# The front and the end of a mixture-of-experts stage: a skewed router, earlier weights, a list of places from batched 16-bit one-hots, and the last bias added per tile

## The chip, the core and the metric

The program runs on one core of a Trainium2 chip. The metric is device time in microseconds (us) of the whole program, the median of several executions. The engines are PE (TensorE, matrix products into the accumulators called PSUM; "PEld" is its weight load), DVE (VectorE), ACT (ScalarE), POOL (GpSimd) and SP (SyncE, which here only issues transfers). Transfers (DMA) are issued from the queues of SP, ACT and POOL; each engine works through its own queue in order.

## What is computed

A two-layer network on 4096 rows of 256 numbers with a 4096 x 4096 adjacency matrix. Each layer is a graph attention and a row-wise network, each added to its input:

```python
x = x + gat0(layernorm(x), adj)
x = x + ffn0(layernorm(x))          # 30 small steps, one 256 x 256 matrix
x = x + gat2(gat1(layernorm(x), adj), adj)
x = x + experts(layernorm(x))
```

The change is in the last line, which in full is

```python
rh = relu(f @ router_w1 + router_b1)
p = softmax(rh @ router_w2 + router_b2)          # 6 experts
top_w, top_i = top_k(p, 2);  r = softmax(top_w)
h1 = relu(f @ w1[e] + b1[e]);  h2 = relu(h1 @ w2[e] + b2[e])
o = h2 @ w3[e] + b3[e]
out = r[0] * o[top_i[0]] + r[1] * o[top_i[1]]
```

The kernel computes only the two experts that each row chose.

## The kernel before

The 4096 rows are 32 tiles (`NT`) of 128 (`P`), and eight groups (`NG`) of four tiles (`G`), 512 rows (`GR`) each. The kernel is a sequence of stages: attention (`attention`, called three times), the 30-step network between the first and second, and the experts. A scheduler of the language orders instructions within a stage on each engine; buffers come from pools, and a tile that takes the memory of an earlier pool waits for that pool's last users.

Four buffers named `rows` (`rows_in`, line 88) carry row groups. `load_ahead` (line 90) loads a group by `rows_of` (line 82), which puts row `r * 128 + p` of the group on partition p: four runs of 1 KB per partition. At the end of an attention, line 577 loads the first three groups of what follows.

The expert stage (lines 755 to 1147) has five parts.

**Router** (lines 761 to 859). All weights of the stage are loaded on ACT's queue when it begins: the router's (`rw1`, `rw2`, `rb2`), the biases as rows (`br`), the last bias (`b3`), and 18 transfers of 256 KB for the experts (`ew`). Then for each group: statistics (line 100 and on), the normalised rows `n` (line 837), their store to DRAM as `nd` (line 840), eight transposes on PE into the one buffer `tp` (line 113), a copy to `fT` on ACT (line 842), four PE instructions of the first product (line 845), `rh` on ACT (line 847), eight for the second (line 850), and the logits `lg` on DVE (line 853). All of a group is written down before the next group. `acc`, the stage's input kept for the residual, is loaded from DRAM a second time (line 859).

**Places** (lines 866 to 955). Softmax, the two greatest, their one-hots `hot`; the count of rows per expert by two products with a triangle and a matrix of ones (lines 896, 897); a running sum over the 32 tiles by doubling (lines 904, 905); and from these each row's place `pos` in a list sorted by expert, with every expert's part filled up to 256 places (`TR`), so 37 tiles (`T`) of 256 in all. `hi` and `lo` are the place's quotient and remainder by 128.

**List** (lines 957 to 979). The list is inverted by products: for each of 64 pairs (choice i, tile t), DVE writes a 128 x 128 one-hot of `lo` (line 961) and a 128 x 74 one-hot of `hi` times a code for the row (line 963), both in fp32, and PE adds their product to `ps_i` (line 966). From the sum come `source` (which row of `nd` to gather) and `dest` (which row of `yd` to scatter to). Beside it, lines 1003 to 1023 make `b3w`, the last bias weighted for each row, by transposing the weights and multiplying with `b3`.

**Experts** (lines 1032 to 1136). For each of 37 tiles: two gathers on POOL (line 1035), transposes (1047), a copy to `xT` on DVE (1049), copies of that tile's expert weights (1063), three layers on PE (1070, 1070, 1091) with `h` on ACT (1081) and on DVE (1083), a copy of the result to `ye` on ACT (1099), and two scatters to `yd` on POOL (1101). The loop is skewed: layer one of tile i, the last layer of tile i - 1, the transposes of tile i + 1, layer two of tile i. Every fourth tile, line 1136 adds a group of `b3w` to `acc`.

**Tail** (lines 1137 to 1147). For each group, two loads of `y` from `yd`, eight multiply-adds on DVE into `acc` (line 1144), and the store of the group; loads and stores are all on SP's queue, in this order.

Of the kernel before, what the change touches and what calls it, by code (L numbers as in the profile page):

```python
# [11 lines left out]
F32 = mybir.dt.float32  # L12
BF16 = mybir.dt.bfloat16
# [8 lines left out]
P = 128  # L22
# [22 lines left out]
def gnn_ffn_kernel(ctx: ExitStack, tc: tile.TileContext, a: dict, out: bass.AP):  # L45
# [44 lines left out]
    def load_ahead(src, g):  # L90
        t = rows_in().rearrange("p (r c) -> p r c", c=C)
        nc.sync.dma_start(t, rows_of(src, g))
        ahead[g] = t
# [77 lines left out]
    def attention(tag, src, norm, w, others, chunks, first, finish, following):  # L171
# [6 lines left out]
        with ExitStack() as scope:  # L178
# [343 lines left out]
            for at, (c, h, q) in enumerate(units):  # L522
# [52 lines left out]
                if at == len(units) - 8:  # L575
                    for g in range(3):
                        load_ahead(following, g)
# [29 lines left out]
    attention("g0", x, True, w0, [make, *makers], [4, 7, 7, 7, 7], True, to_rows(x1d, x), x1d)  # L607
# [128 lines left out]

    for n in range(2):
        attention(
            f"g{n + 1}",
            h1d if n else x2d,  # L740
            not n,
            gw[n],
            [],
            [8, 8, 8, 8],
            False,
            to_rows(x3d, x2d) if n else to_rows(h1d),
            x3d if n else h1d,
        )

# [5 lines left out]
    with ExitStack() as scope:  # L755
# [4 lines left out]
        RH = a["L1_ffn_router_w1"].shape[1]  # L760
        rw1 = one.tile([P, KC, RH], F32, name="rw1")
        nc.scalar.dma_start(rw1, a["L1_ffn_router_w1"].rearrange("(k p) f -> p k f", p=P))
        rw2 = one.tile([RH, E], F32, name="rw2")
        nc.scalar.dma_start(rw2, a["L1_ffn_router_w2"])
        rb2 = one.tile([P, E], F32, name="rb2")
        nc.scalar.dma_start(rb2, bcast_rows(a["L1_ffn_router_b2"]))
        NB = 1 + 2 * KC * E
        br = one.tile([NB, P], F32, name="br")
        nc.scalar.dma_start(br[:1], a["L1_ffn_router_b1"][None, :])
        for i in range(2):  # L770
            at = 1 + i * KC * E
            for k in range(KC):
                nc.scalar.dma_start(
                    br[at + k * E : at + (k + 1) * E], a[f"L1_ffn_expert_b{i + 1}"][:, k * P : (k + 1) * P]
                )
        b3 = one.tile([E, C], F32, name="b3")
        nc.scalar.dma_start(b3, a["L1_ffn_expert_b3"])
        ew = []
        for i in range(3):
            t = one.tile([P, E, KC, C], F32, name=f"ew{i}")  # L780
            src = a[f"L1_ffn_expert_w{i + 1}"]
            for e in range(E):
                nc.scalar.dma_start(t[:, e], src[e].rearrange("(k p) f -> p k f", p=P))
            ew.append(t)
        bT = one.tile([P, NB], F32, name="bT")
        acc = one.tile([P, NT, C], F32, name="acc")
        b3w = one.tile([P, NT, C], F32, name="b3w")
# [4 lines left out]
        source = one.tile([P, T2], I32, name="source")  # L792
        nd = dram.tile([N, C], F32, name="nd")
        yd = dram.tile([2 * N + T * TR, C], F32, name="yd")

        with ExitStack() as rs:
            work = rs.enter_context(tc.tile_pool(name="r_work", bufs=2))
            rone = rs.enter_context(tc.tile_pool(name="r_one", bufs=1))
            psum = rs.enter_context(tc.tile_pool(name="r_ps", bufs=1, space=PSUM))

            def bank(name):
                return psum.tile([P, 512], F32, name=name)


            def numbers(name, pattern, base, step):
                shape = [P] + [n for _, n in pattern]
                ti = rone.tile(shape, I32, name=f"{name}_i")
                nc.gpsimd.iota(ti, pattern=[list(x) for x in pattern], base=base, channel_multiplier=step)
                tf = rone.tile(shape, F32, name=name)
                nc.gpsimd.tensor_copy(tf, ti)  # L810
                return tf

            along = numbers("along", [(1, P)], 0, 0)
            place = numbers("place", [(P, T2)], 0, 1)
            code = numbers("code", [(-N, 2), (-P, NT)], 2 * N, -1)
# [5 lines left out]
            allp = rone.tile([P, P], F32, name="allp")  # L821
            nc.gpsimd.memset(allp, 1.0)

            ps = bank("ps_s")
            nc.tensor.transpose(ps[:, :NB], br, ident[:NB, :NB])
            nc.vector.tensor_copy(bT, ps[:, :NB])
            lg = rone.tile([P, NT, E], F32, name="lg")
            for g in range(NG):
                if g not in ahead:
                    load_ahead(x3d, g)  # L830
                t = ahead.pop(g)
                rstd, mv = over_std(work, t)
                nmr = work.tile([P, G], F32, name="nmr")
                nc.vector.scalar_tensor_tensor(nmr, mv[:, :, 0], -1.0, rstd, op0=OP.mult, op1=OP.mult)
                n = work.tile([P, G, C], F32, name="n")
                for r in range(G):
                    nc.vector.tensor_scalar(
                        n[:, r, :], t[:, r, :], rstd[:, r : r + 1], nmr[:, r : r + 1], op0=OP.mult, op1=OP.add
                    )
                nc.sync.dma_start(rows_of(nd, g), n)  # L840
                fT = work.tile([P, KC, GR], F32, name="fT")
                nc.scalar.copy(fT, transposed(psum, n))
                ps = bank("ps_r")
                for k in range(KC):
                    nc.tensor.matmul(ps[:RH], rw1[:, k, :], fT[:, k, :], start=(k == 0), stop=(k == KC - 1))  # L845
                rh = work.tile([RH, GR], F32, name="rh")
                nc.scalar.activation(rh, ps[:RH], AF.Relu, bias=bT[:RH, 0:1])
                ps = bank("ps_l")
                for r in range(G):
                    nc.tensor.matmul(  # L850
                        ps[:, r * E : (r + 1) * E], rh[:, r * P : (r + 1) * P], rw2, start=True, stop=True
                    )
                nc.vector.tensor_tensor(
                    lg[:, g * G : (g + 1) * G, :],
                    ps[:, : G * E].rearrange("p (r e) -> p r e", e=E),
                    rb2[:, None, :].to_broadcast([P, G, E]),
                    OP.add,
                )
                nc.sync.dma_start(acc[:, g * G : (g + 1) * G, :], rows_of(x3d, g))
# [32 lines left out]
            any_ = rone.tile([P, NT, E], F32, name="any")  # L892
            nc.vector.tensor_tensor(any_, hot[:, 0], hot[:, 1], OP.add)
            flat = any_.rearrange("p t e -> p (t e)")
            psw, pst = bank("ps_w"), bank("ps_t")
            nc.tensor.matmul(psw[:, : NT * E], before, flat, start=True, stop=True)
            nc.tensor.matmul(pst[:, : NT * E], allp, flat, start=True, stop=True)

            upto = [rone.tile([P, NT, E], F32, name=f"upto{i}") for i in range(2)]
            nc.vector.tensor_copy(upto[0], pst[:, : NT * E].rearrange("p (t e) -> p t e", e=E))  # L900
            step, src = 1, 0
            while step < NT:
                x_, y_ = upto[src], upto[1 - src]
                nc.vector.tensor_copy(y_[:, :step], x_[:, :step])
                nc.vector.tensor_tensor(y_[:, step:], x_[:, step:], x_[:, : NT - step], OP.add)
                step, src = 2 * step, 1 - src
            upto, other = upto[src], upto[1 - src]
# [6 lines left out]
                upto[:, NT - 1, :, None].to_broadcast([P, E, N // TR]),  # L914
# [6 lines left out]
            nc.vector.memset(first[:, 0:1], 0.0)  # L921
            for e in range(1, E):
                nc.vector.tensor_tensor(first[:, e : e + 1], first[:, e - 1 : e], tiles[:, e - 1 : e], OP.add)
# [11 lines left out]

            at_ = other
            nc.vector.tensor_tensor(at_, psw[:, : NT * E].rearrange("p (t e) -> p t e", e=E), upto, OP.add)
            nc.vector.tensor_tensor(
                at_, at_, pst[:, : NT * E].rearrange("p (t e) -> p t e", e=E), OP.subtract
            )  # L940
            nc.vector.scalar_tensor_tensor(
                at_, first[:, None, :].to_broadcast([P, NT, E]), float(TR), at_, op0=OP.mult, op1=OP.add
            )
            mine = rone.tile([P, 2, NT, E], F32, name="mine")
            nc.vector.tensor_tensor(mine, hot, at_[:, None].to_broadcast([P, 2, NT, E]), OP.mult)
            pos = rone.tile([P, 2, NT], F32, name="pos")
            nc.vector.tensor_reduce(pos, mine, axis=AX.X, op=OP.add)
            posi = rone.tile([P, 2, NT], I32, name="posi")
            nc.vector.tensor_copy(posi, pos)
            hii = rone.tile([P, 2, NT], I32, name="hii")  # L950
            nc.vector.tensor_scalar(hii, posi, 7, None, op0=OP.arith_shift_right)
            hi = rone.tile([P, 2, NT], F32, name="hi")
            nc.vector.tensor_copy(hi, hii)
# [224 lines left out]
```

## Time and profile before

| what | value |
|---|---|
| time, median of 3 | 3685.03 us (3678.46 to 3688.3) |
| span of the profiled execution | 3686.7 us |
| PE, DVE, ACT, POOL busy over the span | 91%, 81%, 72%, 30% |
| third attention's last matmul ends | 3238.7 us |
| first product of the router (L845) | 3275.7 us |
| last logits of the router (L853) | 3327.6 us |
| first one-hot of the list (L963) | 3346.4 us |
| last product of the list (L966) ends | 3408.0 us |
| first gather (L1035) | 3421.8 us |
| last scatter issued (L1101) | 3642.2 us |

How to read it: the busy shares are averages over all stages and say little of the last 450 us, where the limits change from stage to stage. The rows below the shares cut this part into stages. In the profile's groups a row gives the line, the engine, the operation with the tiles that it writes and reads, the shapes and the count; after the bar the busy time in us and the mean of one in ns; after the second bar the engine's idle time just ahead of these instructions, and what ended it. An fp32 product shows as two PE instructions. In tables by stretch, the granted clock of PE is a share of its full clock.

### The profile page before, as it was taken

The numbers are of one execution on the slowest core, as the hardware profiler recorded it, in microseconds if no ns is written. First come the engines' busy times: TensorE is split into PE (matmuls) and PEld (weight loads), VectorE is DVE, ScalarE is ACT, GpSimd is POOL, SyncE is SP. The second block draws the span as 40 slices with busy tenths as digits, with TensorE's granted clock in tenths as the row PEclk, the third lists the DMA queues.
The fourth block names the chain that finished last, engine by engine and source line by source line (L and its number), as shares of the span: only waits on it lengthen the run. The fifth ranks groups of instructions, "written<-read, shape, count | busy, mean of one in ns | idle before, by whom it ended". The sixth has DMA issues, their size and how long they took to land. (4 is left out here: it accounts for less than half of the span.)

```text
span 3686.7 us, 81508 instructions
## 1 busy us (share of the span) xinstructions
PE 3337.6 (91%) x33683; PEld 3024.9 (82%) x33683; DVE 3004.0 (81%) x6140; ACT 2641.2 (72%) x2947; POOL 1098.3 (30%) x892
## 2 busy tenths in 40 slices
PE   6889999988999999999988999999799999957994
PEld 5788898876888888888877989898688888835784
DVE  6899999988877777877777999999899999945334
ACT  2688888977666666666647999998799999921331
POOL 3211010007877777777730000000000000010672
PEclk8899999989999999999998999999999999975897
DMA  6897796411000000000051223030313313050225
GB/s 135 144 224 166 167 205 127 149 27 38 1 1 1 1 1 1 1 1 1 1 183 42 68 81 124 25 113 29 123 35 123 121 42 122 25 170 1 80 95 174
DMA packets 299656, 291.92 MB, mean 79 GB/s; under 512 B 97267, under 2 KB 255126, under 8 KB 299286
## 3 DMA queue, kind: packets, MB, share of 16 engines
q1 hardware_dynamic: 213856, 226.91, 18.9%
q0 software_dynamic: 73920, 52.97, 9.3%
q10 hardware_dynamic: 11510, 6.85, 0.7%
q8 instruction: 265, 4.34, 0.5%
q14 instruction: 105, 0.86, 0.1%
HBM read 251.42 MB, written 68.81 MB: 87 GB/s over the span
## 5 line engine op out<-in xcount | busy, mean ns | idle before, releaser
L565 PE MATMUL acc<-vals,m 128*128 128x130 f16 (+1 forms) x24576 | 1724.5, 231 | 127.8 <-DVE u L475 88.5
L565 PEld LDWEIGHTS <-m 128*128 128x128 bf16 x24576 | 1623.1, 98 | 215.2 <-issue 94.7
L464 ACT ACTIVATE st<-f1b,f2b 128x1024 bf16<-128x1024 f32 (+2 forms) x1664 | 1660.2, 1071 | 151.0 <-DVE m L533 143.4
L533 DVE TENSOR_TENSOR m<-st,m 128x2048 bf16<-128x2048 bf16 (+2 forms) x832 | 937.2, 1136 | 35.7 <-PE acc L565 28.2
L708 PE MATMUL po<-wT,zT 128*128 128x256 f32 x3840 | 874.7, 381 | 10.6 <-ACT zT L734 10.6
L708 PEld LDWEIGHTS po<-wT,zT 128*128 128x128 f32 x3840 | 714.4, 191 | 100.5 <-ACT zT L734 12.5
L694 POOL TENSOR_TENSOR th<-th,y 128x1024 f32<-128x1024 f32 x240 | 568.1, 2368 | 195.9 <-ACT th L693 195.2
L538 DVE TENSOR_TENSOR m<-m,m 128x2048 bf16<-128x2048 bf16 (+2 forms) x520 | 592.3, 1139 | 25.1 <-PE tp_m L217 0.5
L105 POOL TENSOR_TENSOR ln_rstd<-ln_rstd,mhalf 128x4 f32<-128x4 f32 x272 | 281.7, 1036 | 925.7 <-DVE ln_rstd L104 902.5
L100 DVE BATCH_NORM_STATS2 ln_st<-z 128x6 f32<-128x256 f32 x960 | 337.8, 413 | 191.3 <-ACT z L699 191.3
L734 ACT COPY zT<-tp 128x1024 f32<-128x1024 f32 x240 | 242.8, 1012 | 326.6 <-PE tp L113 326.6
L718 DVE SCALAR_TENSOR_TENSOR y<-po,ln_rstd,bias 128x256 f32<-128x256 f32 x928 | 378.7, 469 | 6.5 <-PE po L708 5.7
L699 ACT ACTIVATE z<-th 128x1024 f32<-128x1024 f32 x240 | 254.4, 1060 | 16.2 <-POOL th L694 16.2
L113 PE MATMUL tp<-ident,z 128*128 128x128 f32 x1920 | 251.9, 275 | 12.8 <-ACT z L699 12.8
L113 PEld LDWEIGHTS tp<-ident,z 128*128 128x128 f32 x1920 | 226.4, 142 | 39.7 <-ACT z L699 16.1
L693 ACT ACTIVATE th<-y 128x1024 f32<-128x1024 f32 x240 | 251.2, 1047 | 4.6 <-DVE y L718 4.5
L207 POOL DMA_DIRECT2D rows<-in_adj_dram x80 | 73.0, 913 | 488.5 <-PE tp_m L217 488.2
L447 POOL MEMSET hs<- 128x4 f32 x3 | 0.3, 103 | 630.1 <-DVE u L488 609.0
L305 PE MATMUL ph<-g_w,xT 128*128 128x264 f32 x384 | 113.5, 457 | 31.0 <-DVE v L375 27.7
L305 PEld LDWEIGHTS ph<-g_w,xT 128*128 128x128 f32 x384 | 85.2, 229 | 51.6 <-issue 16.6
L1035 POOL DMA_INDIRECT gx<-nd,source x74 | 74.6, 1008 | 161.4 <-DVE w L1063 125.2
L475 DVE TENSOR_TENSOR u<-acc,lo 128x520 f32<-128x520 f32 (+1 forms) x104 | 66.5, 653 | 48.4 <-ACT lo L474 48.3
(210 smaller groups left out, 2248.0 us busy)
## 6 DMA issues: line engine op xcount, KB each, us to landing
m<-edges SPq DMA_DIRECT2D x32, 2048.0 KB
rows<-in_adj_dram POOLq DMA_DIRECT2D x64, 448.0 KB, 7.8
edges<-ms SPq DMA_DIRECT2D x64, 448.0 KB
m<-edges SPq DMA_DIRECT2D x16, 1792.0 KB
f1b<-fd SPq DMA_DIRECT2D x32, 512.0 KB
rows<-x1d SPq DMA_DIRECT2D x16, 512.0 KB
y<-yd SPq DMA_DIRECT2D x16, 512.0 KB
f1b<-fd SPq DMA_DIRECT2D x16, 448.0 KB
```

The lines of the kernel that those rows point to most:

```text
L100: nc.vector.bn_stats(st[:, r, :], src[:, r, :])
L105: nc.gpsimd.tensor_tensor(rstd, rstd, mhalf, OP.pow)
L113: nc.tensor.transpose(ps[:, k, r * P : (r + 1) * P], src[:, r, k * P : (k + 1) * P], ident)
L464: nc.scalar.activation(st[:, s, :w], f1b[c, h][:, :w], AF.Relu, bias=f2b[:, 2 * q + s, h : h + 1], scale=BIG)
L533: nc.vector.tensor_tensor(m1[:, :, :w], st[:, :, :w], m, OP.logical_and if turned(q) else OP.min)
L538: nc.vector.tensor_tensor(m2[:, :, :w], m, m1[:, :, :w], OP.subtract)
L565: nc.tensor.matmul(acc[:, i, cols], lhs[:, s, rows], v[:, cols], start=(j == 0 and n_ == 0), stop=(j == NT - 1 and n_ == 1), skip_group_ch ...
L693: nc.scalar.activation(th[at], y[:, g * G : (g + 1) * G, :], AF.Tanh, scale=0.01)
L694: nc.gpsimd.tensor_tensor(th[at], th[at], y[:, g * G : (g + 1) * G, :], OP.add)
L699: nc.scalar.activation(z, th.pop(at - 1), AF.Silu, scale=0.01)
L708: nc.tensor.matmul(po[:, r, :], src[:, k, r * P : (r + 1) * P], wT[:, k, :], start=(k == 0), stop=(k == KC - 1),)
L718: nc.vector.scalar_tensor_tensor(y[:, g * G + r, :], po[:, r, :], rstd[:, r : r + 1], last if end else bias, op0=OP.mult, op1=OP.add,)
```

## The change

- Router: its loop runs over `NG + 2` steps. Step g takes the statistics of group g, the rest up to the transposes of group g - 1, and the products of group g - 2; the transposes have two PSUM buffers. `acc` is made by ACT from the rows in hand, with -1 added, instead of a second load.
- Weights: the router's weights and the bias rows are loaded after the 30-step network in program order, into the memory of the first attention's weights `w0`. The 18 expert loads and `b3` follow the router's loop on SP's queue.
- Rows: `runs_of` replaces `rows_of` for what this stage reads and writes: row `4 p + r` of a group on partition p, one run of 4 KB per partition.
- Places: the running sum is one scan instruction over experts and tiles, in bf16; the starts of the experts' parts are a scan too.
- List: four batches of 16 tiles. Each makes all its one-hots in three DVE instructions, and a row's code is two 16-bit numbers kept as one 32-bit word; PE then does 64 products in fp16.
- Last bias: `b3` is held on all partitions, and DVE adds the tile's row of it where ACT copied the result to `ye`. The weighted bias `b3w` goes, with its products and line 1136.
- Tail: the loads of `y` run up to three groups ahead of the sums (8 buffers for 6), and the stores go to ACT's queue.

The diff, cut to its core:

```diff
+    RH = a["L1_ffn_router_w1"].shape[1]
+    rw1 = w0[:, :, :RH]
+    nc.sync.dma_start(rw1, a["L1_ffn_router_w1"].rearrange("(k p) f -> p k f", p=P))
...
+    def runs_of(t, g):
+        return t[g * GR : (g + 1) * GR, :].rearrange("(p r) c -> p r c", r=G)
...
-            x3d if n else h1d,
+            [x3d, runs_of] if n else [h1d],
...
+            ps_t = rs.enter_context(tc.tile_pool(name="r_pst", bufs=2, space=PSUM))
...
+            for g in range(NG + 2):
+                if 1 <= g and g + 2 < NG and g + 2 not in ahead:
+                    load_ahead(x3d, g + 2, runs_of)
+                if g < NG:
+                    rows[g] = ahead.pop(g)
+                    stds[g] = over_std(work, rows[g])
+                if 2 <= g:
+                    ps = bank("ps_r")
+                    fT = fTs.pop(g - 2)
...
+                    rh = rhs[g - 2] = work.tile([RH, GR], F32, name="rh")
+                    nc.scalar.activation(rh, ps[:RH], AF.Relu, bias=bT[:RH, 0:1])
+                if 1 <= g <= NG:
+                    u = g - 1
...
+                    nc.sync.dma_start(runs_of(nd, u), n)
+                    fT = fTs[u] = work.tile([P, KC, GR], F32, name="fT")
+                    nc.scalar.copy(fT, transposed(ps_t, n))
+                    nc.scalar.activation(acc[:, u * G : (u + 1) * G, :], t, AF.Identity, bias=mone)
...
+            for i in range(3):
+                src = a[f"L1_ffn_expert_w{i + 1}"]
+                for e in range(E):
+                    nc.sync.dma_start(ew[i][:, e], src[e].rearrange("(k p) f -> p k f", p=P))
+            nc.sync.dma_start(b3, bcast_rows(a["L1_ffn_expert_b3"]))
...
-            while step < NT:
-                x_, y_ = upto[src], upto[1 - src]
-                nc.vector.tensor_copy(y_[:, :step], x_[:, :step])
-                nc.vector.tensor_tensor(y_[:, step:], x_[:, step:], x_[:, : NT - step], OP.add)
...
+            nc.vector.tensor_tensor_scan(flat[1], flat[0], flat[0], 0.0, OP.add, OP.max)
...
+            for b in range(2 * NT // HB):
+                i, t0 = b // 2, b % 2 * HB
+                here = slice(t0, t0 + HB)
+                ohl = work.tile([P, P, HB], F16, name="ohl")
+                nc.vector.tensor_tensor(
+                    ohl, along16, lo[:, i, None, here].to_broadcast([P, P, HB]), OP.is_equal
+                )
+                ohh = work.tile([P, T2, HB], F32, name="ohh")
+                nc.vector.tensor_tensor(
+                    ohh, along16[:, :T2], hi[:, i, None, here].to_broadcast([P, T2, HB]), OP.is_equal
+                )
+                nc.vector.tensor_tensor(ohh, ohh, words[:, i, None, here].to_broadcast([P, T2, HB]), OP.mult)
+                two = ohh.bitcast(F16).rearrange("p n (t w) -> p n t w", w=2)
+                for t in range(HB):
+                    nc.tensor.matmul(
+                        psi[:, : 2 * T2],
+                        ohl[:, :, t],
+                        two[:, :, t, :],
...
-            nc.scalar.copy(y, po)
+            nc.vector.tensor_tensor(y, po, b3[:, bass.DynSlice(which[i], 1)].to_broadcast([P, 2, C]), OP.add)
...
-                nc.vector.scalar_tensor_tensor(acc[:, g], b3w[:, g], -1.0, acc[:, g], op0=OP.add, op1=OP.add)
...
+        for g in range(NG + 3):
+            if g < NG:
+                ys[g] = [back(g, i) for i in range(2)]
+            if 3 <= g:
...
+                nc.scalar.dma_start(runs_of(out, g - 3), acc[:, (g - 3) * G : (g - 2) * G, :])
```

## The prediction

> **What bounds the kernel now.** I read the busy table in 40 slices first, then the chain of waits, then a table of stages over the last 450 us, then groups and timeline of each stage. Everything edited here runs after the third attention's last matmul at 3238.7 us, apart from eight small loads. So only this table counts (columns: stretch, its length, busy us and count of PE, PEld, DVE, ACT, POOL, then granted clock, DMA share, GB/s):
>
> ```profile
> 3238.70:3260.00 21.30, 4.75 (x41) 3.30 (x38) 16.51 (x63) 1.84 (x3) 6.07 (x19) 0.61 0.59 181
> 3260.00:3275.60 15.60, 0.00 (x0) 0.00 (x0) 2.02 (x10) 1.00 (x1) 1.01 (x1) 0.50 1.09 360
> ...
> 3310.00:3327.50 17.50, 14.20 (x51) 7.54 (x49) 0.36 (x2) 4.09 (x5) 0.00 (x0) 0.76 0.06 22
> 3327.50:3345.00 17.50, 1.63 (x5) 1.14 (x4) 14.47 (x55) 0.59 (x2) 0.00 (x0) 0.54 0.00 0
> 3345.00:3365.00 20.00, 18.63 (x62) 13.30 (x63) 12.28 (x52) 2.16 (x3) 0.00 (x0) 0.50 0.00 1
> ...
> 3441.00:3500.00 59.00, 59.00 (x294) 51.93 (x293) 24.77 (x45) 21.99 (x43) 41.56 (x42) 1.00 0.29 92
> ...
> 3642.00:3686.70 44.70, 0.00 (x0) 0.00 (x0) 25.95 (x64) 0.00 (x0) 0.97 (x1) 0.51 0.86 287
> ```
>
> Five stages: **router** 3238.7 to 3327.5 (88.8 us; PE does nothing in 3260 to 3275.6 while DMA is full); **places** to the first one-hot at 3346.4 (18.9, DVE alone); **list** to the first gather at 3421.8 (75.4, PE full at half clock); **experts** to the last scatter at 3642.2 (220.4, PE full at full clock); **tail** to 3686.7 (44.5, DMA).
>
> Why the router stands still is in the waits and the timeline:
>
> ```profile
> ACT fT L842 <- DMA ew<-in_L_ffn_expert_w_dram: 26.7, 1, 26.7
> PE ps_r L845 <- DMA ew<-in_L_ffn_expert_w_dram: 21.3, 1, 21.3
> ...
> 3252.36 22.14 ACTq L783 DMA_DIRECT2D ew<-in_L_ffn_expert_w_dram  x18
> ```
>
> The copy fT sits on ACT's queue behind 18 expert-weight issues that took 22 us. Groups for the list and the tail:
>
> ```profile
> L1014 PE MATMUL tp<-b,wT 6*128 6x256 f32 x64 | 36.3, 690 | 1.4 <-ACT wT L1011 1.4
> L966 PE MATMUL ps_i<-ohh,ohl 128*128 128x74 f32 x128 | 35.2, 425 | 0.0
> L1144 DVE SCALAR_TENSOR_TENSOR acc<-y,ws,acc 128x256 f32<-128x256 f32 x64 | 26.0, 479 | 18.2 <-DMA y<-yd 18.2
> ```
>
> The list's PE time is half the list (L966), half the last bias (L1014), which was interleaved with it and also ran on after it until 3420.9.
>
> [...] PE was busy 20.00 of 20 us in 3365 to 3385 and kept 0.50. So I don't count on a full clock. [...] 1218 ns for L533 at 128x2048 bf16 near the end, 690 for 520 fp32 [...]. [...] the trace shows 352 ns for 192 elements, as for tensor_tensor. [...] with 1 KiB rows the tail's middle moved 337 to 374.
>
> **The change part by part.**
>
> *Router, skewed, weights early.* The eight small loads go to SP near 120 us, where SP has room (no issue of its between 117.9 and 124.7): nothing. The expert weights move from ACT to SP: five of 18 ahead of the first nd write, the rest between and behind the nd writes. What is queued behind them on SP is nd and rows; the five are 1.3 MB, 3.6 us at 360 GB/s, and the first nd is not ready sooner than some 5 us after they can start (3245.7, when the first load of that stage starts now). The eight acc loads go; ACT makes acc (128x1024, 1.01 us as L842).
> DVE per group, from its rows divided by 8: statistics 1.50 (L100), 0.38 (L102), 0.17 (L104), 0.16 (L834), n 1.40 (L837), lg 0.18: 3.8 us. Eight groups are 30 us, and the closing of attention on DVE (L475 to L595) 5.7.
> ACT per group: 1.01 + 0.69 + 1.01 = 2.7, hidden.
> PE per group cold: 3.61 (L845 x4) + 1.06 (L850 x8) + 1.7 (L113 x8) = 6.4. Warm, by the FFN's rows: L708 takes 228 ns per 256 columns, so 4 x 512 columns 1.8; transposes 251.9/240 = 1.05; ps_l 0.5: 3.4. Now a period is 6.8 (3301.57 to 3308.38) since fT and rh stand in PE's way; the skew and the second tp buffer remove that. The clock was 0.74 to 0.76 in the last half of the stage; I take 5.3 per group, between 3.8 (DVE) and 6.4 (PE cold).
> The built order has about 17 DVE instructions ahead of n of group 0, so transposes start near 3249; 8 x 5.3 = 42; the last rh, ps_l and lg add 2 to 3: end near **3294**, 33 saved (bounds: 3238.7 + 36 + 3 waits + 6 tail = 3284; 3249 + 51 + 3 = 3303).
>
> *Places.* Ten instructions of the doubling scan (1.6 + 0.9), the PSUM copy (0.4), five of `first` (0.8) and at_ in three go; two scans, a subtraction, the copy of ends, count and shift come. No row shows a scan; [...]. Two matmul groups become four on bf16. ex, ohe, sel and bsel stay in the gaps in the built order. I take 2.3 saved (1 to 4). POOL's constants (2048 elements, about 1.8 us for iota and 1.7 for the cast, extending the rows of 235 and 293 ns at 128) run beside the router.
>
> *List.* Out: 128 DVE one-hots (20.1 + 18.1 us), 128 PE instructions, all of L1009 to L1021. In: four batches, each ohl 2048 elements of 16 bits, 1.2 us [...], ohh 1184 with fp32 output 1.4, and its product 1.4: 4.0, so 16 for four. Of the 64 matmuls only the last 16 come after DVE; [...] I take 3.2. Then lst to source 1.6 (now 2.5), gather 0.6: 16 + 0.7 (ohl waits for PE once) + 3.2 + 1.6 + 0.6 = **22**, against 75.4: 53 saved (bounds 20 and 29). The gather no longer waits for L1014, as PE's last work is the list itself.
>
> *Experts.* PE sets 5.62 per tile: 1.73 + 1.73 + 0.44 + 1.73 by starts at 3501.12, 3502.85, 3504.58, 3506.30, 3506.74. The bias addition replaces ACT's ye (0.59) by about 0.69 on DVE, between w and xT. Queued behind it is xT, for which PE's next first layer waits: po done at 3506.5, ye to 3507.25, xT to 3507.95, needed at 3508.47. Half a microsecond is left, so nothing. L1136 (9.7 us of DVE) goes, hidden but two of eight ahead of source. 0 (from +4 to -2).
>
> *Tail.* 12.6 MB move, 8 MB in, 4 out. Loads now run up to four groups ahead and aren't queued behind stores, which go to ACT's queue; rows are 4 KiB. [...] DVE needs 26 + 4 + 4. From 3644.9 that is 37.5 instead of 41.8: 4.3 saved (1 to 7).
>
> Sum: 33 + 2.3 + 53 + 0 + 4.3 = 93; 3685 - 93 = **3592 us**.
>
> **Rivals.** (A) *Router stays PE-bound and cold, list dearer* [...]: router to 3303, list 29, tail 2: 24 + 1 + 46 + 2 = 73: 3612. For: 0.50 in the list; against: 0.76 in the router and a PE with fewer gaps. (B) *PE warms up and DVE bounds*: router to 3286, list 20, tail 7: 41 + 3 + 55 + 7 = 106: 3579. [...] against: it would then be idle for a third of the time. (C) *ye on DVE joins the loop*: it waits for the scatter of three tiles before, and xT and the next PE work stand behind it. If a scatter's 2.4 us to landing came into each period, 37 x 2.6 = 96 is given back: 3592 + 96 = 3688, slower. For: ACT's ye has 21.0 us of idle put down to that DMA; against: ACT started ye within 0.1 us of po's end, and three tiles are 16.8 us.
>
> **How the numbers follow.** Forecast 0.58, A 0.23, B 0.16, C 0.03. Same needs 3674 to 3696, so most of C falls there or beyond. Range 3568 to 3618: from beyond B, with the 5 us that runs of one kernel differ, to beyond A. Faster 0.97, same 0.01, slower 0.02.
>
> **What would show it.** No idle stretch of PE at the router's start and no wait on ew; eight periods near 5 us at a clock over 0.6; one-hots as 12 DVE rows, ohl near 1.2 us; first gather 88 us earlier, near 3333; 5.62 per tile; a tail under 40 us. Wrong if ew or b3 lands after source, if ohl takes over 2 us, or if a period of the experts grows.

## The result and the profile after

The changed kernel takes **3589.92 us** (median of four runs, 3589.64 to 3591.94), the kernel before beside it 3686.23 (3678.46 to 3688.3). The ratio is 0.9744, with a 95% interval of 0.9727 to 0.9761. The prediction was 3592.

The table of stretches after, with the same columns as before (length, busy us and count of PE, PEld, DVE, ACT, POOL, then granted clock, DMA share, GB/s):

```profile
3240.50:3253.20 12.70, 5.11 (x42) 3.45 (x39) 12.67 (x47) 7.00 (x8) 2.70 (x3) 0.68 0.41 120
3253.20:3265.00 11.80, 10.24 (x31) 6.14 (x31) 6.73 (x28) 3.39 (x4) 9.86 (x25) 0.64 0.68 245
3265.00:3275.00 10.00, 8.98 (x50) 6.07 (x48) 7.02 (x32) 6.00 (x8) 2.30 (x3) 0.97 0.54 191
3275.00:3291.60 16.60, 14.81 (x75) 9.20 (x74) 5.19 (x24) 7.01 (x9) 1.03 (x1) 1.00 0.92 300
3291.60:3307.30 15.70, 0.69 (x4) 0.27 (x4) 14.22 (x45) 0.59 (x2) 0.00 (x0) 0.54 0.13 50
3307.30:3327.70 20.40, 8.86 (x64) 8.22 (x64) 16.84 (x21) 0.80 (x2) 0.01 (x1) 0.58 0.00 1
...
3347.00:3406.00 59.00, 59.00 (x295) 52.09 (x294) 28.68 (x53) 15.92 (x33) 41.40 (x43) 1.00 0.29 94
3548.00:3587.70 39.70, 0.00 (x0) 0.00 (x0) 26.22 (x64) 0.00 (x0) 1.04 (x2) 0.51 0.83 324
```

The stretch in which PE did nothing (3260 to 3275.6 before) is gone: from 3253 on PE is busy for 34 of 38 us, and its clock is at 0.97 or more from 3265. The list is down to one row of 20.40 us, in which DVE is busy for 16.84 and PE for less than half. The experts are as before, 59.00 of 59.00. In the tail 324 GB/s are moved instead of 287.

The waits from 3236 to 3350 (engine and waiting row, releaser, us in total, times, longest) no longer name ew:

```profile
ACT w L1076 <- DVE source L1005: 29.3, 1, 29.3
DVE lg L848 <- PE ps_l L845: 19.2, 8, 4.4
ACT rh L824 <- PE ps_r L822: 18.4, 8, 3.9
PE ps_r L988 <- DVE ohh L985: 15.1, 4, 10.3
...
PE tp L113 <- DVE n L833: 8.0, 7, 4.1
```

In the router DVE and PE now wait for one another: lg, which stands ahead of the next n on DVE, waits for ps_l, and the transposes wait for n. PE's wait on ohh says that DVE now sets the pace of the list. Groups of the tail (L1160), the experts (L1112) and the list:

```profile
L1160 DVE SCALAR_TENSOR_TENSOR acc<-y,ws,acc 128x256 f32<-128x256 f32 x64 | 26.2, 479 | 10.8 <-DMA y<-yd 10.6
L1112 DVE TENSOR_TENSOR ye<-po,b 128x512 f32<-128x512 f32 x37 | 25.6, 692 | 48.2 <-DMA yd<-ye,dest 33.7 <-PE po L1104 14.5
...
L988 PE MATMUL ps_r<-ohh,ohl 128*128 128x148 f16 x64 | 8.9, 304 | 15.1 <-DVE ohh L985 15.1
...
L985 DVE TENSOR_TENSOR ohh<-ohh,code 128x1184 f32<-128x1184 f32 x4 | 5.6, 1388 | 0.1
L982 DVE TENSOR_TENSOR ohh<-along,hi 128x1184 f32<-128x1184 f16 x4 | 5.5, 1385 | 0.0
...
L978 DVE TENSOR_TENSOR ohl<-along,lo 128x2048 f16<-128x2048 f16 x4 | 4.9, 1219 | 0.0
```

ohl, whose second operand is broadcast, takes 1219 ns for 2048 elements; L533 in the kernel before, with none, took 1218 for as many. The tail's sums wait 10.8 us instead of 18.2.

To compare runs, each is cut at six marks: the start of ln_st after its last wait for L565 (the end of attention for DVE), the start of lmax, the first one-hot, the first gather, the last scatter, and the span's end. (The prediction put the router's end 0.3 us ahead of lmax's start. It also calls 3238.7 the end of attention's last matmul; PE's records of L565 run on to 3240.5 there, and 3238.7 is the first mark, where DVE's wait for them ends.) Lengths in us, good to 0.1:

| kernel | router | places | list | experts | tail | time; before on the same chip |
|---|---|---|---|---|---|---|
| before | 89.1 | 18.6 | 75.4 | 220.4 | 44.5 | 3686.23 |
| after | 51.3 | 15.5 | 20.4 | 220.7 | 39.3 | 3589.92; 3686.23 |
| unskewed | **56.8** | 15.5 | 20.4 | 230.1 | 38.5 | 3607.63; 3701.52 |
| ew_on_act | **65.0** | 15.5 | 20.5 | 228.5 | 38.4 | 3618.15; 3701.52 |
| list_pairs | 49.1 | 15.5 | **30.7** | 229.3 | 38.3 | 3611.06; 3701.52 |
| rows_1kb | 51.6 | 15.6 | 20.3 | 228.7 | **41.2** | 3600.41; 3701.52 |
| tail_old | 51.4 | 15.5 | 20.4 | 220.5 | **45.5** | 3601.92; 3691.48 |
| ye_on_act | 51.8 | 15.6 | 20.4 | **220.2** | 39.0 | 3593.52; 3691.48 |
| ye_twice | 51.4 | 15.6 | 20.4 | **221.0** | 38.7 | 3587.38; 3691.48 |
| warm_pe | **49.7** | 15.6 | 20.4 | 219.3 | 38.6 | 3592.82; 3691.48 |
| unskewed_act | **75.5** | 15.5 | 20.4 | 229.9 | 39.9 | 3620.21; 3700.3 |
| xT_twice | 49.7 | 15.5 | 20.4 | **233.7** | 39.0 | 3596.16; 3700.3 |
| best | **47.6** | 15.6 | **23.8** | 230.9 | 38.7 | 3593.54; 3700.3 |
| router_old | **85.6** | 15.6 | 20.4 | 220.5 | 39.2 | 3621.42; 3684.84 |

Bold is the stage that an edit touches. All but best and the first two rows are single runs, so totals are not compared, only stages. Two things are seen ahead of any edit. The untouched router of list_pairs, rows_1kb, tail_old, ye_on_act, ye_twice and xT_twice takes 49.1 to 51.8, so a difference of 2 us there is not read as an effect of an edit. And the experts take about 9 us longer in every run on the two chips on which the kernel before takes over 3700: an edit of the experts is compared only with runs of its own chip.

The trace's record of the granted clock shows what goes with the router's spread. In all seven routers of the changed kernel's form the clock rises to 1.00 some 18 us after the first mark. At 49.1 and 49.7 (list_pairs, xT_twice) it stays there; at 51.3 to 51.8 (the changed kernel and the other four) it falls back to 0.50 once more, 3.4 us later and for 3.4 us. Two stretches of the changed kernel, the second of which holds that fall:

```profile
3260.00:3262.00 2.00, 0.96 (x4) 0.63 (x5) 2.00 (x6) 0.59 (x1) 2.00 (x7) 1.00 0.00 0
3262.00:3264.00 2.00, 2.00 (x4) 0.63 (x3) 2.00 (x11) 0.00 (x0) 1.35 (x12) 0.55 0.68 246
```

### The profile page after: what moved, and what is told of

It reads as the page before. It is cut to its first block, busy times and chain, and to the rows that moved or that the text cites. A ratio compares the mean times of both kernels' runs of the same rounds, so it can differ in the third digit from the quotient of the medians.

```text
span 3587.7 us, 81089 instructions
## 1 busy us (share of the span) xinstructions
PE 3264.7 (91%) x33523; PEld 2981.2 (83%) x33523; DVE 3002.9 (84%) x6039; ACT 2615.2 (73%) x2902; POOL 1100.6 (31%) x899
## 3 DMA queue, kind: packets, MB, share of 16 engines
q1 hardware_dynamic: 198770, 224.18, 19.2%
## 5 line engine op out<-in xcount | busy, mean ns | idle before, releaser
L565 PE MATMUL acc<-vals,m 128*128 128x130 f16 (+1 forms) x24576 | 1726.6, 232 | 128.2 <-DVE u L475 89.0
L565 PEld LDWEIGHTS <-m 128*128 128x128 bf16 x24576 | 1625.2, 98 | 215.6 <-issue 95.5
L533 DVE TENSOR_TENSOR m<-st,m 128x2048 bf16<-128x2048 bf16 (+2 forms) x832 | 938.1, 1137 | 37.0 <-PE acc L565 28.4
L708 PE MATMUL po<-wT,zT 128*128 128x256 f32 x3840 | 875.1, 381 | 10.3 <-ACT zT L734 10.1
L708 PEld LDWEIGHTS po<-wT,zT 128*128 128x128 f32 x3840 | 715.8, 192 | 99.8 <-ACT zT L734 12.4
L538 DVE TENSOR_TENSOR m<-m,m 128x2048 bf16<-128x2048 bf16 (+2 forms) x520 | 592.8, 1140 | 25.1 <-PE tp_m L217 0.5
L699 ACT ACTIVATE z<-th 128x1024 f32<-128x1024 f32 x240 | 254.5, 1060 | 18.5 <-POOL th L694 18.2
L1076 ACT COPY w<-ew 128x512 f32 x37 | 22.7, 617 | 132.8 <-PE ph L1083 103.5
```

The source lines that it names most:

```text
L533: nc.vector.tensor_tensor(m1[:, :, :w], st[:, :, :w], m, OP.logical_and if turned(q) else OP.min)
L538: nc.vector.tensor_tensor(m2[:, :, :w], m, m1[:, :, :w], OP.subtract)
L565: nc.tensor.matmul(acc[:, i, cols], lhs[:, s, rows], v[:, cols], start=(j == 0 and n_ == 0), stop=(j == NT - 1 and n_ == 1), skip_group_ch ...
L699: nc.scalar.activation(z, th.pop(at - 1), AF.Silu, scale=0.01)
L708: nc.tensor.matmul(po[:, r, :], src[:, k, r * P : (r + 1) * P], wT[:, k, :], start=(k == 0), stop=(k == KC - 1),)
```

## The experiments

Every edit is made on the changed kernel.

### The router: four parts put back one by one

**unskewed**: before's loop body, with one buffer for the transposes.

```diff
-            for g in range(NG + 2):
-                if g < NG:
-                    stds[g] = over_std(work, rows[g])
...
+            for g in range(NG):
+                rstd, mv = over_std(work, t)
...
+                nc.scalar.copy(fT, transposed(psum, n))
```

> Router loop as one group after the other, with one buffer for the transposes; the early weights, ew on SP's queue and all else stay. Theory (the skew and the second buffer take fT and rh out of PE's way): the period goes back from 4.2 towards the 6.8 us of the kernel before, so the router takes 60 to 66 us instead of 51.1, and the total grows by 9 to 15. Rival 1 (moving the loads off ACT's queue is the whole gain of the router): the router stays at 51 to 54. Rival 2 (the order of the loop is the whole gain): it goes back to about 85.

Measured 56.8 instead of 51.3: 5.5 us (5.0 to 7.7 against all the untouched routers), below what the theory expected and above the first rival. The loop's order, with its second buffer, was worth less than I had thought. The built program of unskewed already has the next group's transposes ahead of ps_l, so part of what the skew does was there without it.

**ew_on_act**: the weights' issues back on ACT's queue, ahead of the router loop.

```diff
+            for i in range(3):
+                src = a[f"L1_ffn_expert_w{i + 1}"]
+                for e in range(E):
+                    nc.scalar.dma_start(ew[i][:, e], src[e].rearrange("(k p) f -> p k f", p=P))
             lg = rone.tile([P, NT, E], F32, name="lg")
...
-                    nc.sync.dma_start(ew[i][:, e], src[e].rearrange("(k p) f -> p k f", p=P))
```

> The 18 expert-weight loads and b3 are issued from ACT's queue ahead of the router loop, as in the kernel before; the skew and the early router weights stay. Theory (fT stands behind the issues on ACT's queue): fT of the first group waits until ACT has issued 18 loads, near 3270 instead of 3252, and the router takes 65 to 72 us instead of 51.1. Rival (the skewed loop hides it): at most 54 us. The other stages keep their lengths within half a microsecond.

Measured 65.0, 13.7 us more: the theory's lower edge. Its waits from 3240 to 3320 show before's chain again, shorter:

```profile
ACT fT L844 <- DMA ew<-in_L_ffn_expert_w_dram: 18.3, 1, 18.3
...
PE ps_r L828 <- ACT fT L844: 12.8, 1, 12.8
```

The two edits together cost 19.2 of the 37.8 us between the kernels, which left half of the router's gain open. So both were undone at once.

**unskewed_act**:

> Both router edits undone at once: one group after the other with one transpose buffer, and the 18 expert-weight loads and b3 issued from ACT's queue ahead of the loop. Alone they cost 5.5 us (56.6 instead of 51.1) and 13.7 (64.8). What still differs from the kernel before are the early router weights and acc made by ACT instead of eight 1 KB-run loads on SP's queue. Theory A (the edits add): 69 to 72 us, and the remaining 17 to 20 up to 88.8 belong to the acc loads and the router weights. Theory B (only the skew lets the second group's DVE and PE work run while fT waits, so both together cost more than the sum): 78 to 88.

Measured 75.5, that is 24.2 us: 5.0 more than the sum of 5.5 and 13.7, between the two theories. Taken from an untouched router of 49.1 instead of 51.3, the excess would be 2.8. So the skew does seem to hide some of the wait. Still 13.6 us were missing to 89.1.

**router_old**: unskewed_act, and acc by DMA.

```diff
-                nc.scalar.activation(acc[:, g * G : (g + 1) * G, :], t, AF.Identity, bias=mone)
...
+                nc.sync.dma_start(acc[:, g * G : (g + 1) * G, :], runs_of(x3d, g))
```

> unskewed_act (75.3 us of router, by the end of attention's last matmul to lmax) with acc loaded again from x3d, eight DMAs of 512 KB on SP's queue inside the loop, instead of being made by ACT from rows; the subtraction of 1 that ACT did on the way is left out of the computation. Of before's router only its weights' place on ACT's queue (7 small issues ahead of ew) is then missing. 13.5 us are left between 75.3 and 88.8. Theory (4.2 MB more at the 350 GB/s that these stretches move are 12 us, and DMA is full while fT waits): 84 to 89. Rival 1 (the acc loads run beside the work, and the router weights' way is what is left): 75 to 78. Rival 2 (half each): 79 to 83.

Measured 85.6, 10.1 us more: the theory. Its waits from 3240 to 3330:

```profile
PE ps_r L831 <- ACT fT L828: 30.7, 8, 22.7
...
ACT fT L828 <- DMA ew<-in_L_ffn_expert_w_dram: 22.7, 1, 22.7
```

In unskewed_act the same wait of fT was 15.9 us; with the eight acc loads it is 22.7, before it was 26.7. DVE's waits for rows grow too, from 7.6 us in all to 12.9. So the acc loads cost their time by slowing other transfers: the weights whose issues hold up ACT, and the rows. The router's 37.8 us then are: order alone 5.5, queue alone 13.7, both together 5.0 on top, acc loads 10.1, and 3.5 that were not taken apart (the small weights on ACT's queue, 1 KB rows). Each is a difference of single runs, which for an untouched router differ by up to 2.7.

### The list: the pairs without the bias products

**list_pairs**:

```diff
-                nc.vector.tensor_tensor(
-                    ohl, along16, lo[:, i, None, here].to_broadcast([P, P, HB]), OP.is_equal
-                )
...
+                    nc.vector.tensor_scalar(ohl, along, lo[:, i, t : t + 1], None, op0=OP.is_equal)
...
+                        ohh, along[:, :T2], hi[:, i, t : t + 1], code[:, i, t : t + 1], op0=OP.is_equal, op1=OP.mult
```

> The list is made from 64 pairs of fp32 one-hots, each with its own two DVE instructions and its fp32 product, as in the kernel before; the products for the last biases (b3w) stay out. Theory (both edits of the list are worth about half of the 55 us): the list takes 42 to 52 us instead of 20.4. Rival 1 (dropping the bias products is nearly all): 22 to 30. Rival 2 (the batches are nearly all): 65 to 75.

Measured 30.7, just above the first rival's range: of the list's 55.0 us, leaving out the bias products gave 44.7 with the pairs as they were, and the 16-bit batches 10.3 after that. The other order, batches with the bias products kept, was not run. An estimate for it: PE would still have the 46.1 us of bias products (below) and the 8.9 us of the new ones, so the batches alone could give at most some 20 of the 75.4 us. Either way the larger part belongs to the bias products, as far as this estimate goes. My theory was wrong, and the groups of this run from 3311.2 to 3342 show why:

```profile
L976 PE MATMUL ps_r<-ohh,ohl 128*128 128x74 f32 x128 | 27.6, 422 | 7.0 <-DVE ohl L971 7.0
...
L973 DVE TENSOR_SCALAR ohh<-along,hi,code 128x74 f32<-128x74 f32 x64 | 20.2, 315 | 0.0
L971 DVE TENSOR_SCALAR ohl<-along,lo 128x128 f32<-128x128 f32 x64 | 17.9, 281 | 0.0
```

The two DVE groups add up to 38.1 us, but the stretch from the first one-hot to the last product is 28.1. The timeline of DVE (start, us) tells how that goes together:

```profile
3335.03 0.32 DVE L973 TENSOR_SCALAR ohh<-along,hi,code 128x74 f32<-128x74 f32 x1
3335.26 0.28 DVE L971 TENSOR_SCALAR ohl<-along,lo 128x128 f32<-128x128 f32 x1
3335.46 0.32 DVE L973 TENSOR_SCALAR ohh<-along,hi,code 128x74 f32<-128x74 f32 x1
```

A pair comes every 0.43 us, while its two durations sum to 0.60: the next instruction starts before the record of the last one ends. A sum of mean durations over small instructions is too high here by 40%. PE is busy for 27.6 of the 28.1 us, so PE sets the pace of the pairs. In the kernel before the same pairs took 61.6 us (3346.4 to 3408.0), since 46.1 us of bias products (L1009, L1014) were interleaved with them and PE ran on with these until 3420.9, which the gather waited for. So the 44.7 are 33.5 in the pairs and 11.2 between the last pair and the gather.

### The tail

**tail_old**: before's loop with the 4 KB runs kept.

```diff
-            y = work.tile([P, G, C], F32, name="y", bufs=8)
+                y = work.tile([P, G, C], F32, name="y", bufs=6)
...
-                nc.scalar.dma_start(runs_of(out, g - 3), acc[:, (g - 3) * G : (g - 2) * G, :])
+            nc.sync.dma_start(runs_of(out, g), acc[:, g * G : (g + 1) * G, :])
```

> The tail's loop as before: six y buffers, the loads of a group then its sums then its store, all on SP's queue; 4 KB runs stay. Theory (order and queue give the gain): the tail takes 43 to 45 us instead of 39.3. Rival (4 KB runs give it): 39 to 41.

**rows_1kb**: the new loop with before's rows.

```diff
-        return t[g * GR : (g + 1) * GR, :].rearrange("(p r) c -> p r c", r=G)
+        return t[g * GR : (g + 1) * GR, :].rearrange("(r p) c -> p r c", p=P)
...
-numbers("code0", [(0, 2 * NG), (1, G)], 0, G)
+numbers("code0", [(0, 2 * NG), (P, G)], 0, 1)
```

> Row r*128+p of a group instead of row 4p+r on partition p, for nd, yd, out and the router's x3d, with the list's code changed to match: runs of 1 KB instead of 4 KB in DRAM, all orders as in the changed kernel. Theory (deeper loads and the stores on another queue give the tail's gain, the length of a run little): the tail stays at 39 to 41 us (39.3 now, 44.5 before). Rival (4 KB runs give it): 43 to 45. The router has spare transfer time either way: 51 to 52.

tail_old measured 45.5 against 38.6 to 39.0 on the same chip, so 6.5 to 6.9 us (just above the theory's 45) for the order of the loads, the two more buffers and the second queue, which were not tried apart. rows_1kb measured 41.2 against 38.3 to 38.5 on its chip, so 2.7 to 2.9 for the length of the rows (just above the theory's 41). The sums' group in the tail of tail_old:

```profile
L1153 DVE SCALAR_TENSOR_TENSOR acc<-y,ws,acc 128x256 f32<-128x256 f32 x64 | 26.0, 479 | 17.1 <-DMA y<-yd 17.1
```

and of rows_1kb:

```profile
L1160 DVE SCALAR_TENSOR_TENSOR acc<-y,ws,acc 128x256 f32<-128x256 f32 x64 | 26.1, 479 | 12.4 <-DMA y<-yd 12.4
```

With the old order DVE waits as long as before (17.1, before 18.2), whatever the rows; with the new order and short rows, 12.4; with both changes 10.8. Long rows in the old order bring nothing (45.5; before 44.5), so the two parts don't add up to the 5.2 us of the stage: the long rows help only with the new order.

### The experts: has ye's addition room on DVE?

**ye_on_act**:

```diff
-            nc.vector.tensor_tensor(y, po, b3[:, bass.DynSlice(which[i], 1)].to_broadcast([P, 2, C]), OP.add)
+            nc.scalar.copy(y, po)
```

> ye is a copy on ACT as before, the last biases are left out of the computation. Theory (PE sets the period; DVE's addition ends half a microsecond before xT is needed): 5.62 us per tile and 220.7 in all stay within 0.5. Rival (the addition on DVE costs something that another gain hid): the experts get 2 to 10 us shorter.

Measured 220.2 instead of 219.3 to 221.0 in the runs beside it: the same, on a chip on which PE never waits for xT. On the two chips with the longer experts (see the end) it was not tried. The wait for DMA that stands in ye's row (33.7 us) costs nothing: in the changed kernel ye starts 0.04 us after po's last record ends in all 37 tiles. It comes back in ACT's row here (25.1).

**ye_twice**: the addition written twice.

> The addition of the last bias on DVE is done twice per tile (the same output again), 0.69 us more in front of xT. The slack as read from the trace: xT ends 3357.69, its first reader starts 3358.37, 0.68 us, less some hop of 0.05 to 0.1. Theory: the second addition uses the slack up, so a period grows by 0 to 0.2 us, 0 to 8 us in 37 tiles. Rival 1 (no slack: the trace's order hides a chain): 0.5 to 0.7 us per tile, 18 to 26 us. Rival 2 (much more slack than read): exactly 0.

Measured 221.0, no growth, but this run told nothing of the slack. Its timeline (start, us) from 3400:

```profile
3404.56 0.69 DVE L1112 TENSOR_TENSOR ye<-po,b 128x512 f32<-128x512 f32 x1 [1.16 <-DMA yd<-ye,dest]
...
3405.16 0.68 DVE L1062 COPY xT<-pt 128x512 f32<-128x512 f32 x1
3405.76 0.68 DVE L1113 TENSOR_TENSOR ye<-po,b 128x512 f32<-128x512 f32 x1
```

In the built program the second addition stands behind xT, so xT does not wait for it. A second copy of xT can't be moved out of the chain:

**xT_twice**:

```diff
             nc.vector.tensor_copy(xT[i], pt)
+            nc.vector.tensor_copy(xT[i], pt)
```

> xT is copied from PSUM twice per tile by DVE, 0.68 us more in the chain from pt and ye to PE's next first layer, which no reordering can take out of it. Doing ye twice did not test this, because in the built order its second addition stands behind xT. Theory (the slack is the 0.68 us between xT's end and the first matmul that reads it, less a hop of 0.2 as PE starts 0.2 us after its last release elsewhere): 0.1 to 0.3 us per tile, 3 to 11 us in 37 tiles. Rival (no more slack than 0.1): 0.55 to 0.7 per tile, 20 to 26. Rival 2 (all of it hidden): 0.

Measured 233.7 against 229.9 and 230.9 on the same chip: 3.3 us over their mean, 0.09 per tile, for 0.68 us more in the chain. About 0.6 us of each was hidden: the lower edge of the theory, and the half microsecond read from the trace was there. The size is rough, for two reasons. On this chip PE waits for xT in some tiles without any edit. And the built order on PE moved after all: part of a tile's transposes stand behind layer two, just ahead of the first layer that reads xT (at 3450.08 and 3455.80, for example), and fill some of the time.

### Better than the change?

**warm_pe**: PE kept busy ahead of the router.

```diff
+            ps = bank("ps_l")
+            for q in range(14):
+                nc.tensor.transpose(ps[:, q % 4 * P : (q % 4 + 1) * P], ident, ident)
+
             lg = rone.tile([P, NT, E], F32, name="lg")
```

> 14 transposes of the identity, read by nobody, on PE between the transpose of the biases and those of group 0, about 3244.4 to 3248.5. Theory (the first two router groups run at a clock of 0.64 because PE was idle from 3242 to 3248.5; the DVE addition lg behind ps_l holds n of the next group): the first two periods (8.2 and 5.8) shrink by 2 to 5 us in all, and the router takes 46 to 49 us. Rival (PE goes cold again in the gaps of the first group, or the clock needs longer to rise): 50.5 to 52.

Measured 49.7, inside what the untouched router varies by: inconclusive as a gain. Stretches of this run (columns as above) say what the clock did:

```profile
3254.00:3256.00 2.00, 1.03 (x5) 0.38 (x3) 2.00 (x7) 2.00 (x3) 1.01 (x1) 0.83 0.44 143
3256.00:3258.00 2.00, 0.80 (x5) 0.50 (x5) 2.00 (x6) 2.00 (x3) 0.00 (x0) 1.00 0.97 315
3258.00:3260.00 2.00, 0.84 (x5) 0.45 (x4) 2.00 (x12) 1.54 (x2) 0.55 (x1) 0.53 1.13 329
3260.00:3264.00 4.00, 4.00 (x8) 1.83 (x9) 2.06 (x11) 0.45 (x1) 2.33 (x3) 0.50 1.03 382
```

The clock, at 0.50 from 3251.3, did rise to 1.00 at 3254.7, as the 14 transposes ended, but at 3258.1, after PE had been busy for 1.83 of the 4 us from 3254, it fell to 0.50, and the first ps_r (3259.7) ran at 0.50. That is the rival's mechanism, though the stage is shorter than its 50.5 to 52. So **best** fills the gaps of group 0 too (19 transposes in all), lets lg come one group later, and takes the list's second one-hot in fp16:

```diff
-                ohh = work.tile([P, T2, HB], F32, name="ohh")
+                oh = work.tile([P, T2, HB], F16, name="oh")
...
-                nc.vector.tensor_tensor(ohh, ohh, words[:, i, None, here].to_broadcast([P, T2, HB]), OP.mult)
-                two = ohh.bitcast(F16).rearrange("p n (t w) -> p n t w", w=2)
+                two = work.tile([P, 2, T2, HB], F16, name="two")
+                for w in range(2):
+                    nc.vector.tensor_tensor(
+                        two[:, w], oh, code[:, w, i, None, here].to_broadcast([P, T2, HB]), OP.mult
+                    )
...
-                        two[:, :, t, :],
+                        two[:, :, :, t],
```

> Three edits on the changed kernel. Router: 19 unread transposes of the identity ahead of and between those of group 0 so that PE's clock is up for the first groups, and the addition lg one group later in the loop, so DVE waits less for ps_l: 51.1 should become 43 to 48 us (rival: the clock drops again at the next gap, as in warm_pe, where it fell to 0.50 at 3258 and 3271: 49 to 51). List: one-hot ohh in fp16 and two fp16 products with the two code words instead of an fp32 one-hot and an fp32 product, per batch 3 x about 0.72 instead of 1.39 + 1.39: 20.4 should become 17 to 18.5 (rival: matmuls on the new layout are slower by what DVE gains: 19.5 to 21). In all 3581 to 3587, a ratio to the kernel before near 0.972.

Measured 3593.54 (3589.06 to 3608.68, five runs) against 3700.3 for the kernel before on that chip: ratio 0.9721, interval 0.970 to 0.9741. That overlaps the change's own interval, so best is not shown to be faster. By stages the router gained, to 47.6 us, 1.5 below the lowest untouched one; which of its two router edits did it was not tried apart. The list lost 3.4 us, more than the rival allowed for. Stretches of best, router's middle and list:

```profile
3250.00:3258.00 8.00, 6.09 (x34) 4.09 (x34) 6.80 (x22) 4.81 (x5) 7.54 (x23) 1.00 0.58 216
3258.00:3266.00 8.00, 7.86 (x45) 5.38 (x44) 6.84 (x33) 5.16 (x6) 2.13 (x2) 1.00 0.64 238
...
3297.00:3320.70 23.70, 17.75 (x64) 9.46 (x64) 14.58 (x24) 0.76 (x2) 0.00 (x0) 0.50 0.00 0
```

In the router the clock held at 1.00 from 3250 on. In the list DVE is busy 2.3 us less than after (14.58, was 16.84), but PE's 64 matmuls take 17.75 us instead of 8.86, 277 ns each instead of 138. What changed for PE is the step of its moving operand: in best single fp16 values 32 bytes apart, 148 of them, and in the changed kernel 74 pairs 64 bytes apart. In best that is 1.87 ns per place read. In the changed kernel the matmuls of a batch follow each other every 127 ns, 1.7 per pair (the 138 include the start of each batch), and there the weight loads, 139 to 148 ns each, may set the pace as well. The clock is not the reason: the first three of the changed kernel's four batches ran at 0.50 and took 2.19 to 2.22 us each, and the last, for its second half at 1.00, took 2.23. Contiguous fp16 was not tried, so that the step is the cause was not shown.

## Why the prediction was right, point by point

The stages of the two profiles differ by 37.8 + 3.1 + 55.0 - 0.3 + 5.2 = 100.8 us; attention, untouched, ended 1.8 later, which gives the 99.0 between the spans. The prediction's sum was 93.

- **Router: 33 forecast, 37.8 measured.** The cause was right in the main; three terms were off in size, and partly cancel. The transposes start 8.0 us after the first mark instead of 10.3. The eight periods are 4.93 on average instead of 5.3, 3.0 us in all: group starts of ps_r are 3253.2, 3261.4, 3267.2, 3271.8, 3276.1, 3279.7, 3284.1, 3287.7, thus 8.2 and 5.8 while the clock was at 0.50 or went up and down, then 4.1 at 0.97 to 1.00. One clock for the whole stage describes neither kind, so that the average came out near 5.3 is in part luck. What stands around the eight periods took 3.8 us instead of 2 to 3. Rival B's mechanism, a warm PE, held for six of eight groups; its end at 3286 did not come, since the first two were cold, as in rival A. The text named the wait of fT behind ew's issues as the cause, and the runs bear it out as the largest single part, but alone it is 13.7 of 37.8. That "the eight acc loads go" was mentioned without a price: they were worth 10.1.
- **Places: 2.3 forecast, 3.1 measured**, inside 1 to 4. The scan took 0.56 us for 192 elements, where DVE's reductions of lg and its other instructions on it took 0.35 to 0.36 in the kernel before. Not priced: any, written in bf16 across its rows, took 1.01 us.
- **List: 22 forecast, 20.4 measured.** ohl 1.22, ohh 1.39, product 1.39, as priced (1.4 for 1184 elements was an estimate: a line through the 352 ns of 192 and the 690 of 520 in the kernel before gives 1.37). The last 16 matmuls took 2.2 us instead of 3.2, an estimate that rested on no trace, and ohl never waited for PE (0.7 forecast). What the prediction did not ask is which edit gives it: by list_pairs four fifths of this gain come from what was left out of PE's queue, and by the estimate for the other order still more than three fifths, not from the batches that the edit seems to be about.
- **Experts: 0 forecast, 0.3 more measured.** ye_on_act shows that on this kind of chip the engine of ye does not matter, xT_twice that there is slack. Rival C's 96 us did not come. Its order, PE behind xT behind a late ye, does appear on the two other chips and costs some 9 us there, but what holds ye up there is, by the profile, not the scatter (see the end).
- **Tail: 4.3 forecast, 5.2 measured.** Of the reasons given, loading ahead with the stores on another queue is worth 6.5 to 6.9 when taken away, the 4 KB rows 2.7 to 2.9. From the first load (3550.9) to the end the stage took 36.8 us, of 37.5 forecast; 12.6 MB over all of that are 342 GB/s. That 4 KB rows would move more than the 337 to 374 GB/s of the tail's middle before, no trace had shown; in 3555 to 3580 of the changed kernel 397 were moved.
- **What would show it**: no wait on ew, twelve one-hot rows with ohl at 1.22 us, the first gather at 3327.7 (94 us earlier; 88 was forecast), 5.62 us per tile, a tail of 39.3: all as written. Two signs were not: the eight periods are not near 5 us but of two kinds, and PE does stand idle at the router's start, for 1.85 and 4.14 us, on DVE's u and n and not on ew.

## What to carry to other kernels

Read who shares a queue before pricing an operation: the router lost its time to issues on ACT's queue and to loads beside them, and the list to unrelated products in PE's queue, and in both the visible edit (skew, batches) was by itself the smaller part. When two parts of a change each hide the other's cost, undo them together as well as apart: 5.5 and 13.7 became 24.2. And check in the built order that an experiment is where you think it is: ye_twice tested nothing because its second addition had moved behind the work that it should have delayed.

## What the runs showed of the hardware that I had not expected

- **PE's clock fell without a long gap.** In warm_pe it fell from 1.00 to 0.50 at 3258.1, after PE had been 46% busy from 3254 to 3258, with no single gap over 1.0 us. In the other direction, list_pairs kept PE busy for 27.6 of 30.7 us with fp32 products of 74 columns, and the clock stayed at 0.50. So in these two runs the busy share alone did not tell what the clock would do.
- **The clock changed on a beat of 3.41 us.** In warm_pe's record of the granted clock the changes lie at 3251.28, 3254.69, 3258.10, 3264.93, 3271.76 and 3275.17 us, each one or two times 3.41 us after the last. In the kernel before it went up or down every 3.41 us from 3294.60 to 3328.73, and the router's period of 6.81 us (3301.57 to 3308.38), which the prediction put down to fT and rh, is two of these beats. One beat more or less at 0.50 is what goes with the 2 us between untouched routers.
- **Durations of small DVE instructions overlapped** in list_pairs: 0.28 and 0.32 us by their records, one every 0.21 us by their starts.
- **A moving operand with a step**: in best PE took 1.87 ns for each 2-byte place 32 bytes from the next, in the changed kernel 1.7 for each 4-byte pair 64 bytes from the next. With the one-hot's width halved, the list's matmuls took 17.75 us instead of 8.86.
- **Chips differ in one stage**: on two of the chips the experts took 228.5 to 230.9 us in six runs whose experts are the changed kernel's, on the others 219.3 to 221.0, at a granted clock of 1.00 on both. In these six runs ye starts 0.85 to 1.66 us after the end of po's last record in 14 or 15 of the 37 tiles, nearly always every second one; in the other runs of these experts it is 0.04 throughout. With ye xT comes late, and PE waits for it. One such tile of best, where po's record ends at 3457.37 and the next first layer starts at 3459.80:

```profile
3458.45 0.69 DVE L1139 TENSOR_TENSOR ye<-po,b 128x512 f32<-128x512 f32 x1 [2.20 <-PE pt L1087]
...
3459.06 0.68 DVE L1089 COPY xT<-pt 128x512 f32<-128x512 f32 x1
```

  From its transposes to the next ones (3457.20 to 3463.35) this tile takes 6.15 us instead of 5.62; 15 such tiles make 8 us of the 9. The profile names a signal of PE as what released ye, and not a scatter. Why it comes late on these chips stays open, and so does whether ye on ACT would be better there.
